# RWKV values in two halves: the lower half is taken from the PSUM bank or from the copied value

## The chip, the cores and the metric

The kernel runs on one core of one Trainium2 chip. The metric is the device time of one execution in microseconds; of several runs the median is taken. Five engines work side by side, each through its own list of instructions in order: TensorE (PE in the profile; PEld is its weight load), VectorE (DVE), ScalarE (ACT), GpSimd (POOL) and the queue that issues most transfers (SP). They wait for each other by semaphores.

## The reference, cut to what matters

Four layers follow each other on x of shape (16, 100, 512): a cross attention, an RWKV block, another cross attention with a feed-forward part, and a second RWKV block. The change lies in the RWKV blocks:

```python
xm = xa[:, :, None] + sx[:, :, None] * (maa_stack + xxx)
xk, xw, xv, xr, xg = (xm[:, :, j] for j in range(5))
w = jnp.exp(-jnp.exp(time_decay + jnp.tanh(xw @ td_w1) @ td_w2)).reshape(b, l, h, s_)
r = (xr @ Wr.T).reshape(b, l, h, s_)
k = (xk @ Wk.T).reshape(b, l, h, s_)
v = (xv @ Wv.T).reshape(b, l, h, s_)
g = jax.nn.silu(xg @ Wg.T)
def step(s, rkvw):
    r_t, k_t, v_t, w_t = rkvw
    a = k_t[..., :, None] * v_t[..., None, :]
    out = jnp.einsum('bhi,bhij->bhj', r_t, u * a + s)
    s = a + w_t[..., :, None] * s
    return (s, out)
```

There are 32 heads of 16 channels, 100 steps, and 16 sequences.

## The kernel before

Channels lie on the partitions: the 512 channels are four chunks of 128. The 16 sequences are four groups of four, so a tile of one chunk and one group is 128 x 400. Group g and chunk c make one of 16 pieces C of the recurrence, and each piece has eight units of two state columns; 128 units in all in one layer.

A unit goes through four engines. PE spreads the values of two columns over the heads into a PSUM bank (`spread`, tile vb, read from xc). DVE copies the start state into vb and multiplies by the keys (`product`), then runs two scans over the steps (`scan`, tile a). POOL multiplies the scans by r (also tile a), and PE gathers them into the bank acc (`gather`).

PE's spread multiplies by zeros and ones, in a format with a shorter mantissa (fp32r). So that the values come through whole, v is split into an upper half hi, v rounded to that format, and a lower half lo, v - hi; the spread's 128 rows hold both. For each of the four chunks of each group, `plain` and `split` (lines 1050 to 1071) do this: PE makes the product v in a PSUM bank mm by four matrix products over the chunks; ACT copies it to a staging tile v and issues its store to DRAM; ACT copies it once more to hi, rounding it, and issues that store; DVE makes lo by one subtraction, and SP issues its store. Later `enter` loads all of them back for the recurrence. There are 16 such subtractions in a layer and two RWKV layers, so 32.

Three PSUM banks (mm0 to mm2) serve all projections in turn, through `Slots`. A reader on DVE is not recorded at once, but one unit later (`read_later`), or, if the bank comes round earlier, just before it is given out again (`bank`). The subtraction goes through `read_later` as well, with the bank of v as its key:

```python
lows[co] = slots.read_later(ps, low)
```

The projections of the next group are cut into pieces and woven between the units by a written-out schedule: every engine keeps the order in which the instructions are recorded (`InOrder`, `pin`). Group 0 has no units beside it; groups 1, 2 and 3 are made while the units of the group before run. So the order of the work around the subtraction is fixed by the schedule, and the waits follow from who reads and writes which tile. Staging tiles (`stage`) are six buffers in turn. All operations recorded through `InOrder` carry line 89 in the profile and all its matrix products line 94, so tiles tell them apart.

Of the kernel before, what the change touches and what calls it, by code (L numbers as in the profile page):

```python
# [10 lines left out]
F32R = mybir.dt.float32r  # L11
# [3 lines left out]
ALU = mybir.AluOpType  # L15
# [6 lines left out]
T = G * L  # L22
# [15 lines left out]
def xattn_sequence(ctx: ExitStack, tc: tile.TileContext, d: dict, out: bass.AP):  # L38
# [52 lines left out]
    vector, scalar, gpsimd = InOrder(nc.vector), InOrder(nc.scalar), InOrder(nc.gpsimd)  # L91
# [609 lines left out]
    def rwkv(n, ws, small, first, next_weights, last):  # L701
# [6 lines left out]
        with ExitStack() as es:  # L708
# [215 lines left out]
            def projections(g, base):  # L924
# [6 lines left out]
                def store(t, c, tile):  # L931
                    (nc.sync if t in ("lo", "g") else scalar).dma_start(out=to[t][c], in_=tile)
# [109 lines left out]
                def linear(f, w, co, read, tag):  # L1042

                    before = mixes[f] if f >= 0 else soon
                    x = lambda c: xj[f][:, c, :] if f >= 0 else st["xm"][:, c, :]
                    chain(2.7, late, tag, before, lambda ps: ps[:, :T],
                          lambda c: w[:, c, co * 128 : (co + 1) * 128], x, read)
# [3 lines left out]
                def plain(f, w, t, co):  # L1051
                    def read(ps):
                        out = stage(f"{t}_{nm}_{co}")
                        scalar.copy(out[:, :T], ps[:, :T])
                        store(t, co, out[:, :T])
                        if t == "v":
                            split(ps, out[:, :T])

                    def split(ps, v):

                        hi = stage(f"hi_{nm}_{co}")[:, :T]
                        scalar.copy(hi.bitcast(F32R), ps[:, :T])
                        store("hi", co, hi)

                        lo = stage(f"lo_{nm}_{co}")[:, :T]

                        def low():
                            vector.tensor_tensor(lo.bitcast(F32R), v, hi, ALU.subtract)
                            store("lo", co, lo)

                        lows[co] = slots.read_later(ps, low)

                    linear(f, ws[w], co, read, ("in", g, co if t == "r" else 0))
# [873 lines left out]
```

## Time and profile before

| | |
|---|---|
| median of 3 runs | 3131.18 us (3127.56 to 3131.5) |
| profiled execution | 3127.86 us, its span 3126.1 us |
| busy in the span | PE 2858.8, DVE 1675.5, ACT 1308.6, POOL 1159.3 us |
| first RWKV layer, recurrence | about 760 to 1300 us of the span |
| second RWKV layer, recurrence | about 2520 to 3050 us |
| mean granted TensorE clock | 0.961 |

A line of the profile's groups gives the source line, the engine, the operation, the tiles out<-in (buffer numbers left out), the shape and the count; then busy time and mean duration; then the engine's idle time before these instructions and what ended it. A line of the order of time gives start and length in microseconds from the span's start, and in brackets the idle time before it with its releaser. The page's chain of work that ended last is followed back from the last instruction, and gives shares of the span.

### The profile page before, as it was taken

The page shows a single profiled execution, that of the slowest core. Times are in us where ns is not written, and L with a number is a line of the kernel's source. Part 1 is how long each engine was busy: PE and PEld are TensorE (multiplying, and loading weights), DVE is VectorE, ACT ScalarE, POOL GpSimd, SP SyncE. Part 2 cuts the span into 40 slices and gives each one's busy share as a digit, 9 for nine tenths or more (in the row PEclk, how much of TensorE's full clock was granted, in tenths as well). Part 3 has the DMA queues.
Part 4 walks back from the last instruction along what each step waited for, and adds up shares of the span by engine and source line. Part 5 has one row for each costly group of instructions (what it writes and reads, how often), then busy time and mean ns, then how long its engine had stood idle before and what let it go on. Part 6 is the DMA issues. An engine that isn't in the chain of part 4 may idle for free. (4 is left out here: it accounts for less than half of the span.)

```text
span 3126.1 us, 44079 instructions
## 1 busy us (share of the span) xinstructions
PE 2858.8 (91%) x16323; PEld 1488.0 (48%) x16323; DVE 1675.5 (54%) x3507; ACT 1308.6 (42%) x2921; POOL 1159.3 (37%) x953
## 2 busy tenths in 40 slices
PE   6999999878889999989999999989999789999998
PEld 3555555534344444444555555455555344444444
DVE  2555556553989988433333333331000369998981
ACT  3777677753435355422222232221111335344553
POOL 0111111133777777412222111220000367787771
PEclk9999999989999999989999999999999889999999
DMA  6010101013224353230000001020002323324321
GB/s 196 24 34 24 34 24 37 3 39 116 80 77 129 96 161 87 71 88 21 21 22 21 21 21 34 28 71 11 11 11 62 101 63 106 109 76 155 105 60 56
DMA packets 139561, 195.93 MB, mean 63 GB/s; under 512 B 23974, under 2 KB 106854, under 8 KB 139346
## 3 DMA queue, kind: packets, MB, share of 16 engines
q1 hardware_dynamic: 116306, 160.34, 17.3%
q10 hardware_dynamic: 23040, 32.78, 2.9%
q8 instruction: 128, 2.10, 0.3%
q14 instruction: 87, 0.71, 0.1%
HBM read 117.16 MB, written 49.15 MB: 53 GB/s over the span
## 5 line engine op out<-in xcount | busy, mean ns | idle before, releaser
L89 POOL TENSOR_TENSOR a<-a,rc 128x800 f32<-128x800 f32 x256 | 487.8, 1908 | 175.8 <-DVE a L89 113.1
L89 DVE TENSOR_TENSOR_SCAN a<-wc,vb 128x400 f32<-128x400 f32 x512 | 477.4, 974 | 28.1 <-PE acc L94 2.2
L89 DVE CUSTOM_DVE_ANT_0 pr<-l_sc,mask 100x361 f32<-100x361 f32 x512 | 252.1, 529 | 148.7 <-PE l_sc L94 148.6
L89 ACT ACTIVATE pr<-pr,nm 100x361 f32<-100x361 f32 x512 | 301.2, 593 | 5.8 <-POOL sums L89 3.7
L89 DVE TENSOR_TENSOR vb<-vb,kc 128x792 f32<-128x792 f32 x256 | 253.8, 991 | 8.8
L97 PEld LDWEIGHTS l_pT<-ident,pr 100*121 100x121 f32 x1536 | 193.3, 186 | 104.3 <-issue 50.9
L1639 DVE CUSTOM_DVE_ANT_0 junk<-l2a_sc,mask 100x361 f32<-100x361 f32 x256 | 136.9, 535 | 182.5 <-PE l2a_sc L94 165.0
L94 PE MATMUL vb<-xc,sel 128*128 128x400 f32 x512 | 207.0, 487 | 18.0 <-DVE a L89 17.8
L97 PE MATMUL l_pT<-ident,pr 100*121 100x100 f32 x1536 | 216.4, 276 | 6.2 <-ACT pt L89 4.3
L1675 POOL TENSOR_TENSOR pa<-pt,pt 121x1600 f32<-121x1600 f32 x16 | 57.1, 3570 | 363.7 <-ACT pt L1670 363.7
L89 ACT COPY pt<-l_pT 121x400 f32<-121x400 f32 x256 | 125.1, 489 | 149.5 <-PE l_pT L97 148.5
L1860 DVE TENSOR_TENSOR x<-pb,x 100x512 f32<-100x512 f32 x16 | 12.6, 790 | 319.9 <-DMA pb<-po 310.1
L89 POOL TENSOR_TENSOR xj<-tm,ext 128x400 f32<-128x400 f32 x160 | 153.6, 981 | 80.1 <-DVE tm L89 59.8
L94 PE MATMUL v<-l_v_w,ct 128*121 128x512 f32 x384 | 177.0, 605 | 0.0
L75 PE MATMUL h<-yTb,l_fc 128*128 128x400 f32 x512 | 172.8, 499 | 0.6 <-ACT yTb L343 0.6
L94 PE MATMUL k<-ct,l_k_w 128*128 128x361 f32 x512 | 170.6, 476 | 0.0
L75 PE MATMUL p<-l_proj,h 128*128 128x512 f32 x384 | 165.5, 592 | 0.0
L89 POOL TENSOR_SCALAR ve<-mv 100x1 f32<-100x1 f32 x16 | 3.6, 224 | 409.8 <-DVE mv L89 409.8
L94 PEld LDWEIGHTS vb<-xc,sel 128*128 128x128 f32 x512 | 97.2, 198 | 109.5 <-issue 36.1
L94 PE MATMUL l_sc<-kz,qz 32*100 32x361 f32 x1024 | 112.6, 509 | 36.1 <-DVE nm L89 33.9
L89 DVE COPY pt<-l_pT 121x400 f32<-121x400 f32 x128 | 73.5, 574 | 132.1 <-PE l_pT L97 64.8
L75 PEld LDWEIGHTS h<-yTb,l_fc 128*128 128x128 f32 x512 | 96.9, 190 | 74.3 <-ACT yTb L343 2.5
(298 smaller groups left out, 5158.0 us busy)
## 6 DMA issues: line engine op xcount, KB each, us to landing
ct<-in_ctxT SPq DMA_DIRECT2D x32, 722.0 KB
dk<-k ACTq DMA_DIRECT2D x32, 200.0 KB
kc<-dk SPq DMA_DIRECT2D x32, 200.0 KB
dv<-v ACTq DMA_DIRECT2D x32, 200.0 KB
dhi<-hi ACTq DMA_DIRECT2D x32, 200.0 KB
dlo<-lo SPq DMA_DIRECT2D x32, 200.0 KB
vc<-dv SPq DMA_DIRECT2D x32, 200.0 KB
dw<-wd ACTq DMA_DIRECT2D x32, 200.0 KB
```

The costliest lines, as they stand in the source:

```text
L75: nc.tensor.matmul(out=ps, lhsT=lhs(c), rhs=rhs(c), start=(c == 0), stop=(c == n - 1))
L89: return lambda *args, **kw: tc.keep_in_program_order(op(*args, **kw))
L94: pin(nc.tensor.matmul(**kw))
L97: pin(nc.tensor.transpose(out, in_, ident))
L1639: nc.vector.tensor_tensor_reduce(out=junk, in0=ss[r][:L, :S2], in1=t["mask"], scale=-1.0, scalar=FLT_MAX, op0=ALU.add, op1=ALU.min, accum_ ...
L1675: nc.gpsimd.tensor_tensor(t["pa"], t["pt"][0], pt, ALU.add)
L1860: nc.vector.tensor_tensor(x, pb[:, i, :], x, ALU.add)
```

## The change

The subtraction reads the value from the PSUM bank instead of from its copy in SBUF. Its other input, hi, and its output, lo, stay as they are. The copy of v is still made, since v is stored to DRAM for the recurrence.

```diff
                         if t == "v":
-                            split(ps, out[:, :T])
-
-                    def split(ps, v):
+                            split(ps)
+
+                    def split(ps):
 
                         hi = stage(f"hi_{nm}_{co}")[:, :T]
                         scalar.copy(hi.bitcast(F32R), ps[:, :T])
...
                         def low():
-                            vector.tensor_tensor(lo.bitcast(F32R), v, hi, ALU.subtract)
+                            vector.tensor_tensor(lo.bitcast(F32R), ps[:, :T], hi, ALU.subtract)
                             store("lo", co, lo)
 
                         lows[co] = slots.read_later(ps, low)
```

## The prediction

> **What bounds the kernel now.** I read the page first. Its chain of work that ended last lies with TensorE for 12% of the span and with VectorE for 4%, in a thousand short pieces; no single engine carries it. The change touches one subtraction, so I asked for that tile, for the stages around it, and then for the order of time at the places where it runs.
>
> The stages, as busy time by engine in stretches of time (span from, span to, length, then PE, PEld, DVE, ACT, POOL busy, granted clock, DMA share, GB/s):
>
> ```profile
> 820.00:1180.00 360.00, 327.98 (x1370) 159.22 (x1369) 324.08 (x454) 166.32 (x302) 275.20 (x215) 0.96 0.37 114
> 2570.00:2930.00 360.00, 329.45 (x1357) 161.12 (x1357) 323.50 (x454) 166.04 (x302) 274.14 (x211) 0.95 0.35 109
> ```
>
> In these two stretches (the recurrence of the two RWKV layers, with the projections of the next batch groups woven in) PE is busy 91%, DVE 90%, POOL 76%. PE and DVE wait for each other in turn; either can be last. Who waits for whom there:
>
> ```profile
> PE mm L94 <- DVE tm L89: 6.0, 8, 1.2
> PE mm L94 <- ACT hi L89: 3.3, 3, 2.2
> PE mm L94 <- DVE rk L89: 3.2, 3, 1.6
> DVE vb L89 <- PE vb L94: 12.9, 8, 6.0
> DVE tm L89 <- PE mm L94: 4.4, 4, 1.9
> ```
>
> The tile itself, and beside it the nearest row to what it becomes, a subtraction's sister that reads one PSUM bank and one SBUF tile of the same shape (duration in ns: least, median, most):
>
> ```profile
> L89 DVE TENSOR_TENSOR lo<-v,hi x32: 549/612/3915, 728.1 to 2867.2; 128x400 fp32r<-128x400 f32 x32
> L89 DVE TENSOR_TENSOR rk<-mm,vc x13: 548/549/566, 773.4 to 1171.1; 128x400 f32<-128x400 f32 x13
> ```
>
> The subtraction takes 549 ns alone and up to 3915 ns. The order of time shows why (start, length, engine; idle time and its releaser in brackets):
>
> ```profile
> 857.94 4.30 PE L94 MATMUL mm<-xj,l_Wr 128*128 128x400 f32 x12
> ...
> 858.73 1.03 POOL L89 TENSOR_TENSOR gc<-gc,og 128x400 f32<-128x400 f32 x1
> ...
> 859.11 3.92 DVE L89 TENSOR_TENSOR lo<-v,hi 128x400 fp32r<-128x400 f32 x1
> 859.72 1.88 POOL L89 TENSOR_TENSOR a<-a,rc 128x800 f32<-128x800 f32 x1
> ...
> 861.56 1.04 POOL L89 TENSOR_TENSOR rk<-rc,rk 128x400 f32<-128x400 f32 x1
> ...
> 866.70 0.63 PE L94 MATMUL vb<-xc,sel 128*128 128x400 f32 x2 [1.75 <-DVE a L89]
> ...
> 870.33 0.94 PE L94 MATMUL mm<-xj,l_Wr 128*128 128x400 f32 x2 [1.64 <-DVE rk L89]
> ```
>
> The subtraction ends 0.43 us after the last of three POOL operations (863.03 against 862.60). While it has two SBUF inputs it stands still behind POOL. And PE wrote the same bank again at 857.94, 1.2 us before the subtraction began: before the change the bank was free once ScalarE's hi had read it (857.89). That is the change's other side.
>
> In group 0, where the recurrence has not begun, the same three follow each other without a pause:
>
> ```profile
> 727.60 0.49 ACT L89 CAST hi<-mm 128x400 fp32r<-128x400 f32 x1 [0.40 <-ACT v L89]
> ...
> 728.12 0.58 DVE L89 TENSOR_TENSOR lo<-v,hi 128x400 fp32r<-128x400 f32 x1 [6.21 <-ACT hi L89]
> ...
> 728.14 2.95 PE L94 MATMUL mm<-xj,l_Wv 128*128 128x400 f32 x8 [0.23 <-ACT hi L89]
> ```
>
> There PE starts on the bank as soon as hi has ended, beside the subtraction.
>
> **The change part by part.** *The operation.* 32 subtractions, 37.36 us in all. From PSUM I price one at 0.55 us (the rk rows, 13 of them with POOL at work, at most 566 ns); where it follows a wait, in group 0, at 0.575 as it is now. The other end is the tm rows (PSUM and SBUF inputs, but two operations in one) at 0.62, 2 us over all 32. I take 0.55, the same operation. DVE gets back 37.4 - 32 x 0.55 = 19.8 us: 6.5 of it in group 1 of each layer, 3.0 in group 2, 0.1 each in groups 0 and 3.
>
> The Trainium skill ("Perfetto Trace Analysis", Optimizing Scalar/DVE Operations) speaks against the change: about 60 ns of overhead for DVE on SBUF, about 125 on PSUM. That would be 65 ns x 32 = 2.1 us more, an estimate from that page; the rows (549 unstalled from SBUF, 549 from PSUM) show no such difference, and I follow the rows. The skill ("SBUF — State Buffer", Who interferes with whom) also says that the second of two such instructions is blocked until the first finishes. By that, the subtraction at 859.11 would have gone on at 859.76 and the change could win 0.6 us there, not 3.4; the row shows that it lost to three in turn.
>
> *The wait that is added.* PE's next product into the bank of v now waits for the subtraction, not for hi. In the changed program this holds for the next writer at nearly all 32 places; the order on PE, DVE, ACT and POOL is unchanged. Queued behind that product on PE are the spreads into vb and the gathers into acc, so DVE's copy of the start state (12.9 us of waits on PE's vb) is who waits. The hold is the subtraction's start + 0.55 + 0.05 us of release (PE starts 0.05 after hi ends: 728.09, 728.14), less PE's old start:
> - Group 0: 0.60 at each of four places.
> - Group 1: 1.55 (subtraction at 837.52, PE at 836.57), 0.16, 0.58, 1.77 (859.11, 857.94).
> - Group 2: 0, 1.84, 1.78, 0.34.
> - Group 3: 0.60, 1.26, 1.14, 0; in the second RWKV layer 0.60, 1.76, 1.51, 0.
>
> Over both layers 28 us of holds against 19.8 us of gain on DVE. Neither lands whole: a hold is lost in the next PE gap that DVE's work ended, if DVE has come forward, and a later hold shrinks by what DVE has banked. So I walk each group, once per layer:
> - Group 0: DVE idles for 3.6 to 6.2 us before each subtraction and gains nothing; v, hi, subtraction and next product follow each other, 4 x 0.60 = 2.4. Two PE gaps (0.53 until hi, 0.96 until ew, which ACT reached late because of junk_a) could close and leave 1.2.
> - Group 1: 1.55, less the gaps until rk (0.64) and tm (0.63): 0.3 late. The second hold is covered by the 1.55 gained. The third subtraction follows hi directly, 0.58 more. The fourth adds 1.77, about 2.6 late; then the gaps 1.75 and 1.64, both until DVE work that the 3.4 us gained bring forward, close: 0.8 ahead.
> - Group 2: 1.84 less 0.91 banked is 0.93, and the next gap, until rk, is 0.93. The third hold is covered by 0.9 + 1.55 gained. The last, 0.34, meets a gap of 0.31. Nothing.
> - Group 3: DVE gains nothing. 0.60, then 1.16 in its place (a later end, not a sum), less a gap of 0.55 until ew if it closes, then 1.14 in its place: 1.1 if it closes, about 1.7 if not; in the second layer 1.3, or 2.1.
>
> If every gap closes: 2 x (1.2 - 0.8 + 0) + 1.1 + 1.3 = 3.2 us later. If none does: 2 x (2.4 + 3.9 + 1.3) + 1.2 + 1.7 = 18 us. The gaps that DVE's work ended I count as closing; those that ACT ended I do not, since ACT's hi and ew read PE products that are late themselves: 3.2 + 2.4 (group 0) + 1.4 (group 3) = 7.0 us.
>
> *What else moves.* ACT's wait for the subtraction (a staging buffer) goes from v's copy to hi, 0.9 us later; it cost 1.8 us in all and can only shrink. On SP's queue the store of one lo (group 3, second chunk) moves behind one more load of gc, and one load of vc too; an issue is 0.33 us, and they are needed several us later, so nothing. If that cover is gone: 4 x 0.33 = 1.3 us. Some seven POOL products a layer that stood 0.17 to 0.36 us behind a subtraction (a at 2.04 to 2.24 us where 1.88 is the rule) get that back; POOL is at 76% and this lies beside the rest.
>
> **The sum.** The profiled execution took 3127.86 us (span 3126.1); with 7.0 it is 3134.9. The median of the three runs is 3131.18, 3.3 above it, and the forecast goes by the median: 3138.2 us, 0.22% slower. A measurement of this kernel can tell about 0.2%, 6.3 us, from no change, so the forecast lies at that edge.
>
> **Rivals.**
> - All gaps close: +3.2 us, 3134.4, within 0.2%. For it: DVE gaps of that size are there, and in group 0 ACT's other work holds PE anyway. Against: it needs ACT not to slip. 0.32.
> - Faster: DVE, not PE, sets the end of the recurrence, and the holds vanish in PE's waits for DVE (20 us of them in 820 to 1180). Then 19.8 comes back less the 4.8 of group 0, which has no such wait: -15, 3116 us. It decides if PE reaches the unit after each subtraction early, as at 866.70. Against: PE is busy just as long as DVE, and DVE waits for vb for 12.9 us. Half the effect would still be faster. 0.14.
> - The change doesn't do what it says: from PSUM the subtraction stands still behind POOL as now. Then the holds grow to the old ends (5.1 us at 859.11, 46 us over all), of which gaps until DVE work eat some 14: +32, 3163 us. Against: the rk rows. 0.04.
>
> **How the numbers follow.** The forecast has 0.50. Slower by over 0.2%: 0.50 + 0.04 = 0.54; within: 0.32; faster: 0.14. The range goes from 3127, beyond full closing by 7 us for a part of the faster case, to 3150, no gap closing and the 0.62 price (18 + 2 us, less 1).
>
> **What would show it.** Right: lo reads mm, all 32 at 0.55 to 0.58 us, DVE's busy time 20 us lower, PE's waits for hi turned into waits for lo, some 15 to 25 us in all, fewer waits of PE for a, rk and tm in group 1, and marks in the first layer that are later after group 0, even after group 1, later after group 3. Wrong: lo still at 1 us or more; PE gaps before vb gone without new ones at lo; or a first recurrence stretch that is shorter than before.

## The result, and the profile after

The changed kernel takes 3135.91 us (median of 12 runs, 3131.84 to 3143.17) against 3129.13 us for the kernel before (12 runs, 3123.51 to 3133.14). The ratio is 1.0024, 95% interval 1.0015 to 1.0033: 4.7 to 10.3 us slower. The forecast, 7.0 us or 0.22%, lies inside; the point is just past the 0.2% edge, as the forecast was.

The profiled execution took 3139.98 us (span 3138.2, mean granted clock 0.958 against 0.961), so the two profiled executions differ by 12.1 us where the medians differ by 6.8. The page's busy line comes first:

```profile
PE 2863.0 (91%) x16323; PEld 1493.6 (48%) x16323; DVE 1658.1 (53%) x3507; ACT 1310.1 (42%) x2921; POOL 1156.7 (37%) x953
```

DVE is 17.4 us less busy than before (1675.5) and the kernel is slower all the same. The same two stretches of the recurrence, by engine:

```profile
820.00:1180.00 360.00, 324.22 (x1364) 159.41 (x1363) 315.06 (x455) 166.45 (x299) 274.11 (x215) 0.96 0.37 114
2570.00:2930.00 360.00, 325.94 (x1353) 159.43 (x1354) 311.29 (x450) 162.63 (x290) 269.46 (x210) 0.94 0.34 107
```

DVE's share falls from 90% to 87%, and PE's falls with it, 91% to 90%. Work taken from DVE has not made PE busier. The waits in 820 to 1180 (total, times, longest) name the reason. Other tiles in these lists: tm (VectorE) and xj (GpSimd) make the mixed input of a projection, rk is the product of r, k and u that VectorE multiplies by v, ew is the decay's exponential on ScalarE.

```profile
PE mm L94 <- DVE lo L89: 11.4, 8, 3.6
PE mm L94 <- DVE tm L89: 6.1, 8, 1.9
DVE vb L89 <- PE vb L94: 14.1, 9, 5.9
DVE lo L89 <- ACT hi L89: 11.5, 7, 2.7
```

The rows of PE's waits for hi (3.3) and for rk (3.2) are gone; 11.4 us of waits for lo stand in their place. DVE, ahead of its work, now waits itself: for hi before the subtraction, and 14.1 us instead of 12.9 for PE's spread into vb. The tile lo, with the waits of its own engine and of those behind it, and the row rk that had priced it:

```profile
L89 DVE TENSOR_TENSOR lo<-mm,hi x32: 548/575/575, 729.9 to 2879.3; 128x400 fp32r<-128x400 f32 x32
...
  ACT hi L89: 65.9, 24
...
  PE mm L94: 32.6, 23
```

```profile
L89 DVE TENSOR_TENSOR rk<-mm,vc x32: 548/549/575, 780.0 to 3025.8; 128x400 f32<-128x400 f32 x32
```

No subtraction is over 0.575 us; the 3.9 us rows are gone. But 24 of the 32 now wait for hi (13 before), since DVE reaches them early, and PE waits for the subtraction at 23 places, 32.6 us in all. In the kernel before, PE waited for hi at 13 places, 11.4 us in all (from its view of the tile hi, among those who waited for it):

```profile
  PE mm L94: 11.4, 13
```

Two places in the order of time. First group 0, and then the stretch of group 1 that the prediction showed (start, length, engine; in brackets the idle time before and what ended it):

```profile
729.36 0.49 ACT L89 CAST hi<-mm 128x400 fp32r<-128x400 f32 x1 [0.40 <-ACT v L89]
...
729.88 0.57 DVE L89 TENSOR_TENSOR lo<-mm,hi 128x400 fp32r<-128x400 f32 x1 [6.21 <-ACT hi L89]
...
730.51 1.27 PE L94 MATMUL mm<-xj,l_Wv 128*128 128x400 f32 x3 [0.84 <-DVE lo L89]
...
859.12 0.49 ACT L89 CAST hi<-mm 128x400 fp32r<-128x400 f32 x1 [0.45 <-ACT v L89]
...
859.64 0.57 DVE L89 TENSOR_TENSOR lo<-mm,hi 128x400 fp32r<-128x400 f32 x1 [2.75 <-ACT hi L89]
...
860.27 0.70 PE L94 MATMUL mm<-zs,w 128*128 128x400 f32 x1 [3.56 <-DVE lo L89]
...
869.04 0.57 DVE L89 TENSOR_TENSOR lo<-mm,hi 128x400 fp32r<-128x400 f32 x1 [1.34 <-ACT hi L89]
...
869.67 3.63 PE L94 MATMUL mm<-xj,l_Wr 128*128 128x400 f32 x10 [0.53 <-DVE lo L89]
...
876.22 0.83 PE L94 MATMUL vb<-xc,sel 128*128 128x400 f32 x2
...
878.38 2.95 PE L94 MATMUL mm<-xj,l_Wr 128*128 128x400 f32 x8
```

In group 0 PE starts 0.05 us after lo ends, and its gap is 0.84 us where 0.23 had stood behind hi: one hold of 0.6. At 860.27 (third chunk of group 1) the gap is 3.56 us where the kernel before had 2.21 until hi:

```profile
851.95 0.45 PE L94 MATMUL mm<-zs,w 128*128 128x400 f32 x1 [2.21 <-ACT hi L89]
```

At 869.67 the subtraction that had taken 3.92 us takes 0.57, and PE is held 0.53. What it pays for comes next: the vb product at 876.22 and the Wr product at 878.38 start without idle time, where the kernel before waited 1.75 us for a and 1.64 us for rk.

### The profile page after: what moved, and what is told of

It reads as the page before. It is cut to its first block, busy times and chain, and to the rows that moved or that the text cites. A ratio compares the mean times of both kernels' runs of the same rounds, so it can differ in the third digit from the quotient of the medians.

```text
span 3138.2 us, 44077 instructions
## 1 busy us (share of the span) xinstructions
PE 2863.0 (91%) x16323; PEld 1493.6 (48%) x16323; DVE 1658.1 (53%) x3507; ACT 1310.1 (42%) x2921; POOL 1156.7 (37%) x953
```

## The experiments

Each ratio is to the kernel before on the same chip (median 3128.53, 3130.39, 3128.52 and 3129.23 us in the four sets), with its 95% interval; the times in us are the ratio's distance from 1 by that median.

**The hold without the gain.** The subtraction stays as it was; a second, tiny operation on VectorE reads two columns of the bank behind it, so the bank is held as long as the stalled subtraction lasts, and 0.15 us more.

```diff
+            tip = one.tile([128, 1], F32, name="tip")
...
                             vector.tensor_tensor(lo.bitcast(F32R), v, hi, ALU.subtract)
+                            vector.tensor_reduce(tip, ps[:, :2], AX.X, ALU.add)
```

> The subtraction stays as before (copied value less upper half, both in SBUF), and after each of the 32 VectorE sums two elements of v's PSUM bank into a scratch column, so that TensorE has to wait for VectorE there as in the changed kernel, while nothing is won on the subtraction. Theory 1 (the change is a hold on the bank, +28 us at its places, less the time in which the subtraction no longer stands behind GpSimd, -20 us): the holds alone, now up to the subtraction's old end; 15 to 30 us slower than before, about 20, and TensorE idles before its next writer of that bank up to 3 to 5 us in group 1. Rival (the wait is hidden, and the loss comes from the subtraction reading PSUM, for instance beside TensorE's writes): 32 x 0.1 us of extra work, at most 3 us slower.

Measured: 3156.10 us, ratio 1.0090 [1.0078, 1.0103]: 28 us slower [24, 32]. The tile tip, and PE's waits in 700 to 1200:

```profile
L89 DVE TENSOR_REDUCE tip<-mm x32: 145/147/154, 726.1 to 2894.5; 128x1 f32<-128x2 f32 x32
```

```profile
PE mm L94 <- DVE vb L89: 17.8, 9, 3.7
...
PE mm L94 <- DVE tip L89: 7.2, 6, 1.9
```

The 32 small reads are 4.7 us of work and cost 28. The row "vb" is a lesson in reading: PE's product into mm has nothing to do with vb. The third chunk of group 1 shows it:

```profile
857.23 0.15 DVE L89 TENSOR_REDUCE tip<-mm 128x1 f32<-128x2 f32 x1
857.30 0.16 DVE L89 COPY vb<-s 128x8 f32<-128x8 f32 x1
...
857.52 0.42 PE L94 MATMUL mm<-zs,w 128*128 128x400 f32 x1 [3.70 <-DVE vb L89]
```

Here tip ended at 857.38 and PE started 0.14 us later. Where the profile names tip as the releaser (866.81, the next chunk), PE also started 0.14 us behind its end. In between lies DVE's next operation, the copy of the start state into vb, and the wait is put down to that.

**The gain without the hold.** The subtraction is left out: two columns of hi are reduced in its place, which keeps the wait for hi, and hi is stored where lo would be.

```diff
-                            vector.tensor_tensor(lo.bitcast(F32R), v, hi, ALU.subtract)
-                            store("lo", co, lo)
+                            vector.tensor_reduce(lo[:, :1], hi[:, :2], AX.X, ALU.add)
+                            store("lo", co, hi)
```

> The subtraction is left out: in its place VectorE sums two elements of hi (so it still waits for hi, and takes about 0.1 us), and the upper half is stored in the lower half's place. The bank is free once hi has read it, as before. This is more than the gain of the change (37 us of VectorE time less 3, instead of 20) without its hold. Theory 1: VectorE comes forward only in groups 1 and 2 of each layer, where its work ends TensorE's gaps (about 7 us a layer); 5 to 12 us faster than before. Rival 1 (VectorE's time is hidden, TensorE sets the end): within 2 us of before. Rival 2 (VectorE sets the end of the recurrence): 20 us faster or more.

Measured: 3116.09 us, ratio 0.9962 [0.9948, 0.9975]: 12 us faster [8, 16]. DVE is spared about 32 us here (37.4 less 32 x 0.155), more than the change spares it, and 12 come through. Paired product by product with the kernel before, PE is idle 11.8 us less in the profiled execution (20.5 us more with the hold alone). So DVE's time in the recurrence is worth something, about a third of what is taken away, and the hold is what the change pays with. The order of some of SP's loads also differs in this build and in those with GpSimd below; what that is worth by itself was not measured.

**VectorE spared, the bank untouched.** The subtraction moves to GpSimd (POOL), still from the copy.

```diff
-                            vector.tensor_tensor(lo.bitcast(F32R), v, hi, ALU.subtract)
+                            gpsimd.tensor_tensor(lo.bitcast(F32R), v, hi, ALU.subtract)
```

> The same subtraction from the copied value, but on GpSimd. No hold on the bank, and VectorE gets all 37 us back; GpSimd gets 32 subtractions of about 1 us (its xj rows, 128x400, take 0.96 to 0.98 us) in groups where it is busy 76%. Theory 1: the gain on VectorE as with the subtraction left out, less what GpSimd's lists are longer where scans wait for it; 2 to 8 us faster than before. Rival (GpSimd's products a set the pace of the recurrence beside the rest): 5 us slower or more, since each of 24 subtractions stands before an a.

Measured: 3120.48 us, ratio 0.9971 [0.9959, 0.9982]: 9 us faster [6, 13], the upper end of what was expected and a little more. The tile lo there:

```profile
L89 POOL TENSOR_TENSOR lo<-v,hi x32: 1027/1034/1061, 729.9 to 2867.0; 128x400 fp32r<-128x400 f32 x32
```

Nearly twice the unstalled time on VectorE, and better for the kernel: the bank is free for PE from hi on, as before the change.

**The change in parts, by group.** First PSUM in groups 1 and 2 alone, then in groups 0 and 3 alone.

```diff
-                            vector.tensor_tensor(lo.bitcast(F32R), v, hi, ALU.subtract)
+                            vector.tensor_tensor(lo.bitcast(F32R), ps[:, :T] if g in (1, 2) else v, hi, ALU.subtract)
```

> The changed subtraction in groups 1 and 2 of each layer only, where it stood behind GpSimd; groups 0 and 3 as before. Theory 1: by the prediction's walk through the groups, the 0.8 us ahead of group 1 and nothing in group 2, so 2 us faster than before to 1 us slower, and the loss of the whole change lies in groups 0 and 3. Rival (the gaps of TensorE do not close, the holds of groups 1 and 2 land): 5 to 10 us slower than before, about as much as the whole change.

Measured: 3127.04 us, ratio 0.9991 [0.9982, 1.0000]: 2.8 us faster, with 0 at the interval's end; the 2 us expected as the best case lie inside it.

```diff
-                            vector.tensor_tensor(lo.bitcast(F32R), v, hi, ALU.subtract)
+                            vector.tensor_tensor(lo.bitcast(F32R), ps[:, :T] if g in (0, 3) else v, hi, ALU.subtract)
```

> The complement of psum_groups_1_2: the changed subtraction in groups 0 and 3 of each layer, where VectorE gains 0.1 us a group, the others as before. Theory 1: the holds alone, 2 x 2.4 us in group 0 and 1.7 and 2.1 in group 3, some of it closed: 5 to 11 us slower than before, the whole loss of the change and what groups 1 and 2 give back. Rival (the two parts do not add, the loss needs both): within 3 us of before.

Measured: 3135.43 us, ratio 1.0017 [1.0006, 1.0028]: 5.3 us slower [1.9, 8.8]. The tile lo has both kinds here:

```profile
L89 DVE TENSOR_TENSOR lo<-mm,hi x16: 548/575/576, 722.9 to 2876.4; 128x400 fp32r<-128x400 f32 x16
L89 DVE TENSOR_TENSOR lo<-v,hi x16: 550/2042/3787, 838.6 to 2744.2; 128x400 fp32r<-128x400 f32 x16
```

The stalls are in groups 1 and 2 (median 2.04 us there in this execution), and the edit loses in groups 0 and 3, where there is next to nothing to win: -2.8 and +5.3 make +2.5, against +7.5 by the ratio of the whole (4.7 to 10.3); the intervals overlap. The parts are not independent, though. With PSUM in groups 0 and 3 alone, PE's idle time fell in group 1, by 2.4 and 1.5 us (first and second layer), and rose in group 2, by 2.3 and 2.2, though the subtraction is as before in both. In the whole change and in this part SP issues one load of gc in each layer ahead of the store of lo instead of behind it, as the prediction saw; no wait of PE in group 3 (1085 to 1150) is for a transfer.

The same split for GpSimd, in groups 1 and 2 and then in groups 0 and 3:

```diff
-                            vector.tensor_tensor(lo.bitcast(F32R), v, hi, ALU.subtract)
+                            (gpsimd if g in (1,2) else vector).tensor_tensor(lo.bitcast(F32R), v, hi, ALU.subtract)
```

> The subtraction runs on GpSimd in groups 1 and 2 only; groups 0 and 3 keep it on VectorE, reading the copy. The whole move gave -9 us and the mix of PSUM in groups 1 and 2 with GpSimd in groups 0 and 3 gave +3. Theory (GpSimd's gain comes where VectorE is near its limit, groups 1 and 2): 6 to 14 us faster than the kernel before. Rival (the gain comes from groups 0 and 3): within 4 us of the kernel before.

Measured: 3121.91 us, ratio 0.9968 [0.9957, 0.9980]: 10 us faster [6, 13].

```diff
-                            vector.tensor_tensor(lo.bitcast(F32R), v, hi, ALU.subtract)
+                            (gpsimd if g in (0,3) else vector).tensor_tensor(lo.bitcast(F32R), v, hi, ALU.subtract)
```

> The subtraction runs on GpSimd in groups 0 and 3 only. Theory (the gain comes from groups 1 and 2): between 2 us faster and 5 us slower than the kernel before; if it adds up with the mixed kernel (+3) and PSUM in groups 1 and 2 alone (-3), 6 us slower. Rival (the gain comes from groups 0 and 3): 5 to 10 us faster; then the mixed kernel's miss lies in how its two halves act on each other.

Measured: 3130.33 us, ratio 1.0000 [0.9990, 1.0010]: no difference. As far as the intervals tell, GpSimd's whole gain comes from groups 1 and 2. There the stalls are gone from VectorE as in the PSUM version (10 against 2.8 us); the 7 us between the two can be the held bank, and the 0.575 us that the PSUM version still takes on VectorE, less what GpSimd's 1.03 us costs. These weren't parted.

**The other way to spare the bank.** hi is rounded from the copy, so that ScalarE's reading of the bank ends with v, one step (0.9 us) earlier.

```diff
-                        scalar.copy(hi.bitcast(F32R), ps[:, :T])
+                        scalar.copy(hi.bitcast(F32R), v)
```

> The upper half is rounded from the copied value in SBUF instead of from the bank; the subtraction is as before. So the bank is free after ScalarE's first copy, about 0.9 us sooner than before the change, the opposite of the change's hold and nothing won on the subtraction. Theory 1: TensorE's waits for hi go (about 2.3 us in group 0 and 3.3 us in groups 1 to 3 of the first layer; some return as waits for the products behind), 3 to 8 us faster than before. Rival (TensorE's waits at these places are hidden): within 2 us of before.

Measured: 3126.28 us, ratio 0.9996 [0.9983, 1.0009]: the same, and the expectation missed. PE's waits in 700 to 1200:

```profile
PE mm L94 <- DVE tm L89: 10.4, 12, 1.9
...
PE mm L94 <- POOL xj L89: 4.4, 4, 1.4
...
PE mm L94 <- ACT ew L89: 3.5, 4, 1.6
```

In the kernel before, the same rows and that of hi were:

```profile
PE mm L94 <- DVE tm L89: 9.6, 12, 1.8
PE vb L94 <- DVE a L89: 8.8, 6, 2.4
PE mm L94 <- ACT hi L89: 6.3, 7, 2.2
...
PE mm L94 <- POOL xj L89: 2.1, 3, 1.2
PE mm L94 <- ACT ew L89: 1.5, 2, 1.0
```

The waits for hi are gone and turn up as waits for tm, xj and ew, together 5.1 us more. PE reaches the same products earlier and finds them no earlier ready. With both edits together:

> A version that may beat both kernels: hi rounded from the copied value (the bank free after ScalarE's first copy), and the subtraction on GpSimd. The subtraction on GpSimd alone gave 9 us, hi from the copy alone nothing that could be told. If the two add where VectorE no longer ends TensorE's gaps: 9 to 14 us faster than before. If TensorE's waits at the bank stay hidden: 7 to 9 us faster, as with the subtraction on GpSimd alone.

3117.42 us, ratio 0.9968 [0.9956, 0.9980], 10 us faster [6, 14], not to be told from GpSimd alone.

**Another order on PE.** The four r products of a chunk are recorded right behind that chunk's v product, so that the next use of v's bank comes later; once with the subtraction from the copy, once from PSUM.

```diff
+                    plain(3, "Wr", "r", c)
...
-                for c in range(NC):
-                    plain(3, "Wr", "r", c)
```

> The pieces of a group's projections in another order: each chunk's product for r (four matrix products, 2.7 us by the schedule's own estimate) directly behind the chunk's v, instead of all four r behind all v; the subtraction as before (from the copied value). So two pieces, not none or one short one, lie between v and the next writer of its bank. It is the partner of the next run; by itself I expect it within 6 us of before on either side, since the same work is done in another order.

Measured: 3155.72 us, ratio 1.0077 [1.0064, 1.0091]: 24 us slower where 6 at most were expected, a miss. The order itself costs that.

> The same order of pieces with the changed subtraction (from the bank). Theory 1: the hold is now mostly covered by r's product, the subtraction still comes free of GpSimd's stalls, so the change that costs 7 us in the old order gains here: 3 to 8 us faster than spaced_sbuf (the run before this). Rival (reading PSUM itself, or something else in the change, costs): 5 to 8 us slower than spaced_sbuf, as in the old order.

Measured: 3148.46 us, ratio 1.0052 [1.0040, 1.0065], 7.3 us less than its partner. PE's waits in 700 to 1200 of this kernel start with

```profile
PE vb L94 <- DVE a L89: 26.5, 14, 5.3
PE mm L94 <- DVE tm L89: 9.1, 10, 1.6
```

and neither lo nor hi is in that list at all. Nor are they in its partner's, which starts with

```profile
PE vb L94 <- DVE a L89: 26.7, 16, 5.1
PE mm L94 <- DVE tm L89: 9.1, 10, 1.6
```

In the kernel before, vb's row has 8.8 us. So in this order PE waits for the recurrence instead of for the bank, and the same edit wins: the subtractions are 15.0 us shorter in all (33.1 and 18.1), of which 7.3 come through. The sign of the edit hangs on the order around the subtraction. The new order both takes PE's wait at the bank away and makes PE wait more for DVE, and these two weren't parted. An order that spaces the bank without this cost wasn't tried.

**A mix.** PSUM in groups 1 and 2, GpSimd in groups 0 and 3.

```diff
-                            vector.tensor_tensor(lo.bitcast(F32R), v, hi, ALU.subtract)
+                            if g in (1, 2):
+                                vector.tensor_tensor(lo.bitcast(F32R), ps[:, :T], hi, ALU.subtract)
+                            else:
+                                gpsimd.tensor_tensor(lo.bitcast(F32R), v, hi, ALU.subtract)
```

> Each group gets what suits it: groups 0 and 3 subtract on GpSimd (no hold on the bank), groups 1 and 2 on VectorE from the bank. From groups 1 and 2 the 3 us that psum_groups_1_2 gave, from 0 and 3 what GpSimd gave there (VectorE gets 18 x 0.6 us back, but its chain is short of work in group 0): 3 to 8 us faster than before. If GpSimd's 9 us came from groups 1 and 2 (TensorE never held, VectorE free), this one is slower than the subtraction on GpSimd everywhere by 3 to 6 us.

Measured: 3129.53 us, ratio 1.0011 [1.0001, 1.0022]: 3 us slower [0, 7], a miss: 3 to 8 us faster was expected, or, by its second case, 3 to 6 us slower than GpSimd everywhere, and by the ratios it is 12. Its halves alone gave -2.8 and 0, so some 6 us, with an uncertainty of 5, are unexplained. It is not the order: every engine's instructions, SP's transfers with them, have the same order as in the half with GpSimd in groups 0 and 3. The profiled execution doesn't show the loss either, as PE is idle 1.4 us less than in the kernel before. The cause stays open.

## Why the prediction was right

- **The operation's price.** 0.55 us forecast, 0.575 where it follows a wait; measured 548 to 575, median 575, because 24 of them now follow a wait. All 32 take 18.3 us, so 37.4 - 18.3 = 19.1 us come back, not 19.8; DVE's busy time fell 17.4. A small miss in size.
- **PSUM's price by the page.** The Trainium skill ("Perfetto Trace Analysis", Optimizing Scalar/DVE Operations) has about 125 ns of overhead for VectorE on PSUM against about 60 on SBUF. The shortest of the two kinds of subtraction in one execution above take 548 ns from PSUM and 550 from SBUF; no run here shows the difference.
- **The wait that is added.** PE's waits for lo were to be 15 to 25 us in all; the row has 32.6, so this sign missed as it was written. The row counts whole waits, with the part that had been a wait for hi (11.4); the added part is 21.2, and it is the added part that the walk reckoned with.
- **The walk by groups.** PE's products come in the same order in both traces. Paired one by one, they give the difference of PE's idle time in each stretch (times of the kernel before):

| stretch, first / second layer | forecast, per layer | measured, us of PE idle |
|---|---|---|
| group 0: 724-760 / 2478-2515 | +2.4 (1.2 if ACT's gaps close) | +1.43 / +1.55 |
| group 1: 826-900 / 2580-2650 | -0.8 | -1.27 / -0.19 |
| group 2: 960-1010 / 2712-2765 | 0 | +0.51 / +0.59 |
| group 3: 1088-1140 / 2840-2900 | 1.7 / 2.1 (1.1 / 1.3 if they close) | +1.10 / +1.67 |

 The sum is 5.4 us where the forecast had 7.0. The signs of groups 0, 1 and 3 hold. The choice that ACT-ended gaps stay open was too dear: groups 0 and 3 together came out nearly 3 us below the forecast, group 0 and the first layer's group 3 near the closed case. Group 2 was too cheap by half a microsecond each. These misses have opposite signs, which helped. And the windows leave out what lies between the groups: over the whole of 820 to 1180 and 2570 to 2930, with group 0, PE's idle time grew by 9.2 us, so 3.8 us stand where the walk had nothing, most of them before products that read xj, in 900 to 1060. The mechanism of the walk held, holds less gaps that close; that the total came within a microsecond of the medians is in part luck.
- **A slip in the sums.** With no gap closing, the walk's own terms for group 3 are 1.7 and 2.1, not the 1.2 and 1.7 that the sum used: 19.0 us, not 18, and a range to 3151. The 7.0 doesn't use them.
- **A term put at nothing.** ACT's wait for a staging buffer, until the store of an earlier lo has landed, was to shrink. In group 3 (second chunk) it went from 1.16 us to none in the first layer, but from 0.67 to 2.41 in the second, and PE's gap behind that subtraction is 2.00 us where the hold was put at 1.76.
- **The gaps that close.** Named ahead: PE's waits for a and rk at 866.70 and 870.33. Both are gone, and rk left the list of waits in 820 to 1180. The waits for tm shrank in group 1 alone (826 to 900: 1.2 us, then 0.6); in 820 to 1180 they are as before (6.0 and 6.1).
- **The rivals.** All gaps closing (+3.2) lies below the interval of 4.7 to 10.3, though groups 0 and 3 went most of that way. The faster case wanted DVE to set the end: the gain without the hold shows 12 us, and the holds ate it and more, as they were not lost in waits for DVE. The third rival (the subtraction stalls as now and holds the bank) was priced at +32; the first experiment comes near that case, with 28 [24, 32].
- **What the forecast did not contain.** Of the 12.1 us between the two profiled executions, 8.1 are idle time of PE, by the same pairing over the whole program; the other 4 are products that ran slower. One stretch shows it, 720 to 760 of the kernel before and of the changed one; the third number from the end is the granted clock:

```profile
720.00:760.00 40.00, 35.78 (x102) 18.37 (x101) 7.25 (x14) 18.89 (x41) 7.16 (x9) 1.00 0.49 162
```

```profile
720.00:760.00 40.00, 34.35 (x88) 16.98 (x86) 7.11 (x13) 16.71 (x37) 8.60 (x11) 0.91 0.45 149
```

 In this stretch PE fell 4.8 us behind, 1.4 of it idle time. The kernel with the subtraction on GpSimd in all groups also has 0.91 there and is faster than the kernel before, so I don't count the clock to the change. That is argued, not shown; the forecast is held against the medians (6.8 us apart), not against these two executions.

## What to carry to other kernels

Before an operation is pointed at a PSUM bank instead of a copy, ask who writes that bank next and when: the reader's end becomes the writer's start, and here 32 reads of 0.15 us, put behind the old ones, cost 28 us. A stall that is shortened on one engine pays only where another engine was waiting for it; split such an edit by stage, since here the edit in the groups with stalls gained 2.8 us (0 at the interval's end) and in those without lost 5.3. If an engine is to be spared, another engine on which the operation takes longer can be the better place: 1.03 us on GpSimd, from the copy, gave 9 to 10 us where 0.575 us from PSUM lost 7.

## What the runs showed of the hardware

- All 16 subtractions of the kernel before that took over 0.6 us ended 0.43 us behind the end of a GpSimd operation, and none of the 32 of the changed kernel, which read PSUM, took over 0.575 us. In 14 of the 16 that was the GpSimd operation in progress when the subtraction began. Where another stood right behind it, the subtraction went on first and that one was longer, as in group 2:

```profile
987.76 1.03 POOL L89 TENSOR_TENSOR og<-og,sq 128x400 f32<-128x400 f32 x1
...
988.10 1.12 DVE L89 TENSOR_TENSOR lo<-v,hi 128x400 fp32r<-128x400 f32 x1
988.75 2.23 POOL L89 TENSOR_TENSOR a<-a,rc 128x800 f32<-128x800 f32 x1
```

 At the two longest (859.11, and 2613.68 in the second layer) it lost to three operations in a row, two of which began after it. The Trainium skill ("SBUF — State Buffer", Who interferes with whom) has the second of two instructions blocked until the first finishes; that fits the 14, and the first of the three alone at the other two. Why those two differ stays open. On GpSimd the same subtraction took 1027 to 1061 ns at all 32 places.
- The release of a bank from VectorE to PE took 0.05 us behind the subtraction (730.46 to 730.51), as from ScalarE, and 0.14 us behind the two-column reduction.
- The mean granted clock lay between 0.955 and 0.966 from one profiled execution to another, and the time tended to go with it (over 76 executions of the kernel before, the correlation of the two is -0.6): with hi from the copy, 3115.8 us at 0.966 where that kernel's median is 3126.3; with hi from the copy and the subtraction on GpSimd, 3127.8 us at 0.956 where the median is 3117.4. By their profiled executions the two would have stood the other way round. In one set of 24, the kernel before ran from 3121.24 to 3137.45 us, so a difference of 10 us between two single executions of these kernels says nothing.
